# A cross-attention block in fp32: the two key halves of the probabilities are added first in 18 of 32 attention units, not 16, and the program's order is laid out anew

## The chip, the cores and the metric

The kernel runs on one core of one Trainium2 chip. The metric is the time of one execution on the device in microseconds (us). Three runs of the kernel before gave 653.56, 655.43 and 656.57 us; their median, 655.43 us, is the time before. The engines are called as the profile calls them: PE (matrix multiplication; PEld is its weight load), DVE (vector engine), ACT (scalar engine), POOL (GpSimd), and SP, which here only issues transfers (DMA). SBUF is the on-chip memory that all engines use, PSUM the banks into which PE writes.

## The reference

One transformer block without self-attention, on x of 8 x 256 x 512 and a context of the same shape, all in fp32, 16 heads of width 32:

```
x1  = layer_norm(x);  q = x1 @ q_w + q_b;  k = ctx @ k_w + k_b;  v = ctx @ v_w + v_b
s   = softmax(q @ k^T / sqrt(32), over the 256 keys)           per batch and head
hid = (s @ v) @ cproj_w + cproj_b + x
out = hid + gelu(layer_norm(hid) @ fc_w + fc_b) @ proj_w + proj_b      inner width 2048
```

The softmax is computed as exp(score - row maximum), then a product with the values, then a division by the row's sum of exponentials.

## The kernel before, in words

**Stages.** The batches are treated in two groups g of four (1024 tokens each). Each group goes through projections (k, v, q), attention, the output projection o, a second layer norm, and the MLP (fc, gelu, proj, named fc and pd). The products of the projections use Strassen's scheme: seven products P1 to P7 instead of eight, where sums of blocks are formed on DVE and POOL before (tiles named ..t or ..i), and the PSUM banks X, Y, W of a product are added into the result by DVE or copied by ACT after (operations named _t, _c). Group 1's projections lie among the attention of group 0, and the attention of group 1 lies among the o and fc products of group 0, so that PE has something else to do while the softmax of a unit runs on the other engines.

**An attention unit** is one batch and four heads, named by three digits: group, head group, batch. So 003 is group 0, head group 0, batch 3; there are 32 units. `scores` (operations s, ev, mx, mc, fold, mf, md, mm, less, exp, ss) makes on PE the scores with keys on the partitions, in two halves kc of 128 keys (8 matmuls that use 32 rows of the array each, "row" form). ACT copies them out with the mask (ev, line 614). DVE finds the row maxima (mx, L1033; fold, L1040; mf, L1042), with three small copies by ACT between (mc, L1039). The maxima are stored to DRAM (md, L594) and loaded back into all partitions (mm, L588). DVE or POOL subtract them (less, L1053 or L1057), ACT takes the exponential (exp, L1060). `attend` (av) then makes the product of probabilities and values, 8 matmuls that use 32 columns ("col" form), and the row sums, as a product with ones. There are two kinds of unit. In a p unit the product with ones runs over both key halves:

```
sums_ = [(lambda j=j: tile_of(av)[j * HD : (j + 1) * HD, 256:512], lambda: ones,
          lambda j=j, kc=kc: at(pt[j // 2], 2 * kc + j % 2), kc == 0) for kc in range(2) for j in range(4)]
```

In a z unit the two halves are first added on DVE or POOL into a tile ss (two operations ss_0, ss_1 of 128 x 512, L625), and the product with ones runs once over the sum, four matmuls in place of eight. The table KINDS says which unit is which, in the order in which the units stand.

**Order, engines and places** are written out by hand in two long tables of words. PROGRAM gives the one order in which all operations are issued, and after a colon the engine of an operation that has a choice (V DVE, A ACT, G POOL). Each engine, SP included, runs its operations strictly in that order; an operation that must wait holds up what stands behind it on its engine. PLACES gives the buffer slot of every tile: a slot holds one tile after the other, and an operation that writes a tile waits until the last reader of the slot's tile before is done. A wait on a slot is as binding as one on data. Tiles of kind Q have an even number and two halves of kind P, so that slot 54 names the Q tile there as well as its first half.

**Weights of the fc and pd products** are loaded again for each group by SP (names fl and pl, lines L588). For the fc product of group g, half s, outer product p, four loads fl{g}{s}{p}_0 to _3 are made: _2 carries the operands of the inner products P5 and P6, _3 those of P7 and P3. So fc011 is the product of group 0, half 1, p = 1; its P6 needs fl011_2, its P7 needs fl011_3.

The profile's line numbers are those of the program below; nearly all products are recorded on line 634, all additions on 625, all loads on 588 and all stores on 594.

Of the kernel before, what the change touches and what calls it, by code (L numbers as in the profile page):

```python
# [122 lines left out]
cq0_00_0 turn_c0_10_0 turn_c0_00_0 vw00 c0_10_0:A c0_00_0:V small v0_0_P1a cq0_00_1 cq0_01_1 vw10 vws3:G cq0_01_0 cq0_11_0  # L123
cq0_11_1 turn_c0_00_1 turn_c0_10_1 c0_00_1:V kw00 c0_10_1:A v0_0_P1b v0_1_P1a turn_c0_11 v0_1_P1b vw11 c0_11:A
turn_c0_01 c0_01:A turn_c0_31 cq0_10_1 cq0_10_0 vws1:G turn_c0_21 kw10 xt0_1 fw0_00_1 fw0_00_0 k0_0_P1 c0_31:A kw11
vw01 c0t1:V v0_0_t1:A vws2:V fw0_11_1 c0_21:A k0_1_P1 c0t2:V rows1 v0_1_t1:A c0t3:V fw0_11_0 turn_c0_30 turn_c0_20
v0_0_P6 xt0_0 fw0i1_3:G rows6 c0_30:V c0_20:A c0t4:V v0_1_P6 fw0i1_1:V v0_0_P2 v0_1_t2:V fw0i1_2:G fw0i4_1:V v0_1_P5
v0_0_t2:A v0_0_P5 fw0i1_4:V v0_0_t3:A kws1:G kws3:G fw0_10_1 stats_x0_00 fw0_10_0 vws4:V rows3 fw0s1:V fw1_00_1
fw0i4_3:G fw0s3:V rows0 rows7 v0_1_t3:A rows2 mk rows8 fw0s2:V rows4 mk~1 v0_1_P2 rows5 v0_0_P3 fw0i4_2:G xt0_4
v0_1_P3 xt0_6 cols kws2:V xt0_3 xt0_5 v0_0_c12:A cols~1 k0_0_t1:A fw0i5_3:V xt0_2 stats_x0_10 fw0i6_3:G fw0i5_1:G  # L130
fw0_01_1 stats_x0_20 fw0i6_1:V stats_x0_11 aggr_x0_11 fw0_01_0 xt0_7 fw0i5_2:G k0_1_t1:A fw1_00_0 fw0i5_4:G fw0i7_1:G
stats_x0_31 kw01 k0_1_P7 fw0i4_4:V fcd0_7_False aggr_x0_31 fw0i7_2:G fw0i6_2:V aggr_x0_00 fw0s4:V k0_0_P6 fw0i3_3:G
fw1_11_1 k0_0_P7 aggr_x0_10 stats_x0_01 aggr_x0_01 k0_1_P6 fw1_01_0 fw1_11_0 fcd0_6_False aggr_x0_20 eps_x0_1 v0_1_c11
stats_x0_30 pow_x0_1 aggr_x0_30 fw0i6_4:G fcd0_6_True k0_0_t2:A k0_0_P5 xt1_3 nb_x0_1 eps_x0_0 k0_1_t2:A k0_1_P5
stats_x0_21 k0_1_P2 fcd0_3_False fcd0_5_True aggr_x0_21 kws4:G k0_0_t3:A fw0i7_3:G eps_x0_3 pow_x0_0 k0_0_c22
k0_1_t3:A fw1i4_1:V eps_x0_2 pow_x0_3 nb_x0_3 fw0i7_4:V qw00 k0_1_c11 k0_0_P3 norm_x0_31:A fw0i2_3:V k0_1_c22 k0_0_P2
k0_1_P3 norm_x0_30:V pow_x0_2 fw1i4_2:V fw0i2_1:V k0_0_c11 norm_x0_10:V norm_x0_11:A fw1_01_1 nb_x0_0 fw1i4_3:V
fw1i4_4:G fw0i2_2:V nb_x0_2 norm_x0_00:V fcd0_1_True v0_1_c12:V k0_0_P4 norm_x0_01:A fw0i2_4:G fcd0_5_False fw1i1_1:G
k0_1_P4 norm_x0_20:A qw10 k0_1_c12:V k0_0_c21 k0_0_c12:A norm_x0_21:A v0_0_c11 turn_x0_10 x0_10:V qw11 fw1i1_3:G
turn_x0_31 fw0i3_1:G turn_x0_00 qw01 turn_x0_11 x0_00:A x0_11:A x0_31:V cb1_12 turn_x0_01 turn_x0_21 turn_x0_30  # L140
turn_x0_20 x0_20:A x0_01:V fcd0_2_True fw1i1_2:V qws1:V fcd1_4_True qws3:G q0_0_P1 fw0i3_2:G x0_21:A fw1i1_4:V x0t1:V
q0_1_P1 cb1_11 x0_30:A q0_0_P2 fw1i2_1:V fw0i3_4:V fw1i2_2:V x0t3:V fw1i2_3:V kd0_0_21 q0_0_t1:A qws2:V q0_0_c11
q0_0_P7 s000 kd0_0_11 kd0_0_12 xt1_2 stats_x1_11 q0_1_t1:A ev000_20 x0t2:V q0_0_P6 fw1_10_0 cb1_03 fw1_10_1
fcd1_1_True cb1_00 ev000_01 x0t4:V cb1_13 fw1i2_4:V ev000_10 fcd0_7_True q0_1_P6 ev000_31 ev000_00 fcd1_2_True
ev000_11 q0_0_t2:A q0_0_P5 q0_0_t3:A ev000_21 fw1s1:V fw1s3:V fw1s2:V fw1s4:V aggr_x1_11 q0_0_c22 ev000_30 mx000_1
q0_1_t2:A cb1_10 fcd0_3_True fcd1_5_False cb1_02 mx000_0 qws4:G fw1i3_1:G mc000_1 mc000_3 q0_1_P2 fw1i7_3:G q0_0_P4
# [1367 lines left out]
```

## Time and profile before

| | before |
|---|---|
| time, median of 3 (us) | 655.43 (653.56 to 656.57) |
| the profiled execution's own time (us) | 654.56 |
| its span, first to last instruction (us) | 652.6 |
| PE busy | 644.3 us (99%) |
| DVE busy | 581.6 us (89%) |
| ACT busy | 346.7 us (53%) |
| POOL busy | 393.5 us (60%) |
| DMA, mean | 144.83 MB, 222 GB/s |

The shares are means over stages of different kinds. A row of the view of groups reads: line, engine, operation, output <- inputs, sizes and count | busy us, mean ns of one | idle time before. A row of the timeline reads: start, length, engine, line, operation, count, and in brackets the idle time before it with what ended it. The granted PE clock is 1.00 in every stretch of the span. A tile's slot can bear the name of the first tile that lay in it, so that a load of fc weights may be printed as a load into xn_y, k or xt.

### The profile page before, as it was taken

Reading aid. Unit: us, or ns where it says so; the run is one execution under the profiler, and the core shown is the slowest. Engines: PE = TensorE matmul, PEld = TensorE weight load, DVE = VectorE, ACT = ScalarE, POOL = GpSimd, SP = SyncE. Lnnn points to the kernel's source line nnn. Section 1 sums busy time; section 2 is a strip of 40 time slices with the busy share of each in tenths; the row PEclk is TensorE's granted clock in tenths of the full one; section 3 lists DMA queues with packets and bytes.
Section 4 is the critical chain, followed back from the end, with each engine's and each line's share of the span. In section 5 each row is a group of like instructions: output and inputs, shape, how many; then the busy total and the mean of one; then the engine's idle time right before and its main releaser. Section 6 shows DMA issues by size and latency. Waiting matters only on the chain.

```text
span 652.6 us, 11265 instructions
## 1 busy us (share of the span) xinstructions
PE 644.3 (99%) x3793; PEld 487.4 (75%) x3793; DVE 581.6 (89%) x981; ACT 346.7 (53%) x711; POOL 393.5 (60%) x355
## 2 busy tenths in 40 slices
PE   9999999999999999999999999999999999999997
PEld 7845454477445676777787888888888888888886
DVE  2889999999989999999999999998878879988676
ACT  3235588999999889865884655030030232632000
POOL 2653687869997897598859765233263334512740
PEclk9999999999999999999999999999999999999999
DMA  8799998679673567786886588989979988567775
GB/s 280 232 341 313 291 263 295 224 207 153 192 237 111 159 213 217 263 264 214 247 252 193 182 262 264 298 282 230 178 196 222 219 228 191 159 171 201 204 131 98
DMA packets 206713, 144.83 MB, mean 222 GB/s; under 512 B 117136, under 2 KB 167104, under 8 KB 206656
## 3 DMA queue, kind: packets, MB, share of 16 engines
q1 hardware_dynamic: 206656, 144.11, 78.1%
q8 instruction: 30, 0.49, 0.3%
q14 instruction: 27, 0.22, 0.1%
HBM read 104.10 MB, written 39.98 MB: 221 GB/s over the span
## 4 chain that ended last, share of the span: by engine, by line
PE 60%; DMA 1%; ACT 0%; DVE 0%; issue 0%
PE fc_X L634 15%; PE pd_X L634 15%; PE fc_W L634 7%; PE pd_W L634 7%; PE pd_Y L634 4%; PE fc_Y L634 4%; PE av L634 2%; PE o_X L634 2%; PE s L634 1%; PE o_W L634 1%; DMA xn_y<-fcd 1%; PE ps_y L722 1%; PE o_Y L634 1%; ACT xn_y L822 0%; PE pd_V L634 0%; PE ps_o L1322 0%
## 5 line engine op out<-in xcount | busy, mean ns | idle before, releaser
L614 ACT ACTIVATE pr<-s,cols 128x256 f32<-128x256 f32 x256 | 103.7, 483 | 19.5 <-PE s L634 17.3
L1057 POOL TENSOR_TENSOR pr<-pr,mm 128x512 f32<-128x512 f32 x72 | 94.2, 1336 | 5.1 <-DMA mm<-md 5.1
L1033 DVE TRANSPOSE_TENSOR_REDUCE mx<-pr 128x32 f32<-128x1024 f32 x64 | 76.8, 1219 | 1.9 <-ACT pr L614 1.7
L1060 ACT ACTIVATE pr<-pr 128x1024 f32<-128x1024 f32 x64 | 66.8, 1067 | 8.9 <-POOL pr L1057 8.1
L1237 ACT ACTIVATE h<-h,cols 128x256 f32<-128x256 f32 x128 | 54.4, 498 | 31.0 <-DVE h L625 30.9
L625 DVE TENSOR_TENSOR h<-fc_X,h 128x512 f32<-128x512 f32 x80 | 52.3, 674 | 4.9 <-PE fc_X L634 4.5
L625 POOL TENSOR_TENSOR ss<-pr 128x512 f32<-128x512 f32 x24 | 32.0, 1344 | 15.4 <-ACT pr L1060 13.8
L625 DVE TENSOR_TENSOR h<-fc_W,h 128x512 f32<-128x512 f32 x48 | 31.8, 676 | 5.3 <-PE fc_W L634 5.1
L1053 DVE TENSOR_TENSOR pr<-pr,mm 128x1024 f32<-128x1024 f32 x28 | 35.2, 1275 | 0.0
L1039 ACT COPY mx<-mx 32x64 f32<-32x64 f32 x96 | 23.3, 243 | 12.2 <-DVE mx L1033 10.7
L623 POOL TENSOR_TENSOR z1i<-h,z1i 128x512 f32<-128x512 f32 x8 | 10.8, 1367 | 21.8 <-PE pd_X L634 16.4
L601 ACT COPY h<-fc_X 128x512 f32<-128x512 f32 x13 | 7.5, 593 | 29.6 <-PE fc_X L634 29.6
L634 PE MATMUL fc_W<-y1i,fl 128*128 128x256 f32 x88 | 22.1, 379 | 0.0
L1040 DVE TENSOR_REDUCE mx<-mx 32x32 f32<-32x256 f32 x32 | 18.5, 578 | 3.3 <-ACT mx L1039 3.1
L606 ACT ACTIVATE e<-pd_X,cols 128x256 f32<-128x256 f32 x7 | 3.3, 473 | 32.5 <-PE pd_X L634 32.5
L634 PE MATMUL pd_X<-z0i,pl 128*128 128x256 f32 x88 | 20.3, 379 | 0.0
L811 POOL TENSOR_TENSOR rs_y<-rs_y,neg_half 128x2 f32<-128x2 f32 x8 | 7.3, 918 | 18.7 <-DVE rs_y L808 11.4
L634 PEld LDWEIGHTS fc_W<-y1i,fl 128*128 128x128 f32 x88 | 16.7, 190 | 2.3
L634 PEld LDWEIGHTS pd_X<-z0i,pl 128*128 128x128 f32 x88 | 16.7, 190 | 2.3
L634 PE MATMUL fc_X<-y1i,fl 128*128 128x256 f32 x72 | 18.1, 381 | 0.0
L1428 POOL TENSOR_TENSOR hid<-hid,cb 128x1024 f32<-128x1024 f32 x6 | 16.5, 2768 | 2.5 <-DVE a1t L625 1.8
L625 DVE TENSOR_TENSOR po<-pd_W,po 128x256 f32<-128x256 f32 x24 | 9.9, 413 | 9.0 <-PE pd_W L634 8.9
(619 smaller groups left out, 1861.9 us busy)
## 6 DMA issues: line engine op xcount, KB each, us to landing
mm<-md SPq DMA_DIRECT2D x32, 512.0 KB, 4.6
pl<-prd SPq DMA_DIRECT2D x49, 256.0 KB, 3.5
fl<-fcd SPq DMA_DIRECT2D x46, 256.0 KB, 3.7
fw<-in_L_xattn_fc_w_dram SPq DMA_DIRECT2D x16, 256.0 KB, 6.5
hid<-in_x_dram SPq DMA_DIRECT2D x8, 512.0 KB, 3.7
pw<-in_L_xattn_proj_w_dram SPq DMA_DIRECT2D x32, 128.0 KB, 3.8
hd<-hid SPq DMA_DIRECT2D x8, 512.0 KB, 4.7
fcd<-fw0i SPq DMA_DIRECT2D x7, 512.0 KB, 5.2
```

The costliest lines, as they stand in the source:

```text
L614: lambda e: nc.scalar.activation(to(), of_(), AF.Identity, bias=bias(), scale=1.0))
L623: nc.gpsimd.tensor_tensor(to()[:, ts(k, 512)], in0()[:, ts(k, 512)], in1()[:, ts(k, 512)], op)
L625: E[e].tensor_tensor(to(), in0(), in1(), op)
L634: nc.tensor.matmul(o(), l(), r(), start=first, stop=True, skip_group_check=True)
L1033: T.op(f"mx{u}_{h}", [("DVE", 1.126)], [(pr[h], None)], [(mx, [h])], lambda e, h=h: nc.vector.tensor_reduce(tile_of(mx)[:, 0:64].rearrange ...
L1039: lambda e, a=a: nc.scalar.copy(tile_of(mx)[0:32, 64 * a : 64 + 64 * a], tile_of(mx)[32 * a : 32 * a + 32, 0:64]))
L1040: T.op(f"fold{u}", [("DVE", 0.38)], [(mx, [0, 1, 2, 3, 4])], [(mx, [5])], lambda e: nc.vector.tensor_reduce(tile_of(mx)[0:32, 256:288], ti ...
L1053: nc.vector.tensor_tensor(p_, p_, m_[:, None, :].to_broadcast([P, 2, 512]), ALU.subtract)
L1057: E[e].tensor_tensor(p_, p_, m_, ALU.subtract)
L1060: lambda e, h=h: nc.scalar.activation(tile_of(pr[h]), tile_of(pr[h]), AF.Exp), table="exp")
L1237: lambda e, f=f, b=b, c=c: nc.scalar.activation(at(h[f][b], c), at(h[f][b], c), AF.Gelu_apprx_tanh, bias=col(c_fcb + f * 4 + c), scale=1.0 ...
L1428: lambda e, v=v: E[e].tensor_tensor(v(), v(), cb.t[:, None, :].to_broadcast([P, 2, D]), ALU.add), lock=True)
```

## The change

Units 003 and 023 (the 11th and 12th of group 0) become z units. That takes 8 matmuls with ones from PE (4 in each), and adds 4 additions of 128 x 512 (ss003_0, ss003_1, ss023_0, ss023_1), all on DVE. The tables PROGRAM and PLACES are written anew as a whole, with the same operations otherwise: of those with a choice of engine 22 go from DVE to ACT, 17 from ACT to DVE, 53 from POOL to DVE and 58 from DVE to POOL. In instructions PE has 8 fewer matmuls, DVE 6 instructions fewer (7 fewer of 128 x 1024), ACT 5 more, POOL 12 more (16 more of 128 x 512, 4 fewer of 128 x 256).

```diff
 PROGRAM = """
...
-q1_1_P4 q1_1_c11 s110 pw0i1_4:G fold122 ev110_10 a0t3:G ev110_20 ev110_01 ev110_11 ev110_00 mx120_1 o0_0_t1 mf122
...
+ss001_0:V ev031_30 less003_1:V xb1_31 xT1_00 v1_1_P3 ev031_31 exp021_0 xb1_32 xb1_30 v1_1_P2 mc011_2 v1_1_c21 mx031_1
+xT1_01 xb1_33 xb1_21 att012 ss021_1:G ev031_00 v1_1_c12:V xb1_20 exp003_1 less003_0:G mc011_1 fold011 x1_00:A v1_0_P4
+exp003_0 x1_01:A v1_0_c21 ss003_1:V av001 ku033 ss003_0:V ss021_0:G ev031_11 ev031_10 s013 mf011 q1_0_P1 xT1_31 xT1_21
...
+q1_1_c11 pw0i1_3:V pw0_10_00 s110 mc122_1 q1_1_P4 mm100 pw0i1_2:V less100_0:V o0_1_t1 mc102_1 mc102_2 mc102_3 fold102
...
 PLACES = """
...
-mv_y0_0=8 rs_y0_0=5 xn_y0_00=51 xn_y0_01=6 st_y0_1=6 mv_y0_1=1 rs_y0_1=9 xn_y0_10=0 xn_y0_11=39 st_y0_2=1 mv_y0_2=7
...
-h0_01=18 fl011_0=83 fl011_1=83 fl011_2=6 fl011_3=18 fc011_X=1 fc011_Y=0 fc011_W=6 fl006_0=16 fl006_1=9 fl006_2=69
...
+mm122=72 av100=7 r100=10 rc100=5 att1_00=42 s110_0=0 s110_1=2 s110_2=3 s110_3=7 pr110_0=54 pr110_1=50 mx110=1 mm110=88
...
+y0i1=78 fc001_X=5 h0_00=58 fc001_Y=6 h0_10=30 fc001_W=2 h0_11=18 h0_01=14 fl011_0=38 fl011_1=74 fl011_2=54 fl011_3=66
...
-KINDS = ("zzzzzzzzzzpppppp", "ppppppppppzzzzzz")
+KINDS = ("zzzzzzzzzzzzpppp", "ppppppppppzzzzzz")
```

What the new order moves is shown at three places.

**DVE, ahead of the scores of unit 110** (the tile that q_1_Y is added into is the q of that unit: operation q1_1_c11; pw0i are weight sums for pd, the row L1053 is less100_0). DVE before:

```order
L1033 TENSOR_REDUCE mx_2247<-pr_0_2174 128x2x16
L625 TENSOR_TENSOR att_11_1287<-av_2205,r_2253 128x256
L625 TENSOR_TENSOR pw0i_2197<-pw_00_2056 128x256
L1053 TENSOR_TENSOR pr_0_1993<-pr_0_1993,mm_2278 128x1024
L625 TENSOR_TENSOR pw0i_2197<-pw0i_2197,pw_00_2056 128x256
L1040 TENSOR_REDUCE mx_2247<-mx_2247 32x32
L625 TENSOR_TENSOR hid_1_2092<-o_1_X,hid_1_2092 128x2x256
L1042 STREAM_TRANSPOSE mx_2247<-mx_2247 32x32
L625 TENSOR_TENSOR xt_3_497<-q_1_Y,xt_3_497 128x512
```

DVE at the same place in the changed order:

```order
L625 TENSOR_TENSOR att_11_1327<-av_2192,r_2237 128x256
L1033 TENSOR_REDUCE mx_2262<-pr_0_2126 128x2x16
L1033 TENSOR_REDUCE mx_2262<-pr_1_2142 128x2x16
L625 TENSOR_TENSOR v_1_21_362<-q_1_Y,v_1_21_362 128x512
L625 TENSOR_TENSOR pw0i_2247<-pw_00_1906 128x256
L625 TENSOR_TENSOR pw0i_2247<-pw0i_2247,pw_00_1906 128x256
L1053 TENSOR_TENSOR pr_0_1982<-pr_0_1982,mm_2303 128x1024
L625 TENSOR_TENSOR hid_1_2190<-o_1_X,hid_1_2190 128x2x256
```

The addition of q_1_Y now stands ahead of the two pw0i sums, the subtraction, the addition into hid and the two small reductions. On PE the scores of unit 110 stand one product earlier, ahead of q1_1_P4 instead of behind it.

**ACT, ahead of the last exponential of unit 033** (L614 on s is ev, L614 on att is the bias ab0, L606 is a copy of a q product; the last row is exp033_1; the rows with pr_0_2063 and pr_1_2109, or pr_0_2126 and pr_1_2142 after the change, belong to unit 122). ACT before:

```order
L614 ACTIVATE pr_0_2063<-s_1_2043,cols 128x256 x2
L1060 ACTIVATE pr_1_1700<-pr_1_1700 128x1024
L606 ACTIVATE kws_368<-q_1_X,cols 128x512
L1039 COPY mx_2076<-mx_2076 32x64 x3
L614 ACTIVATE pr_1_2109<-s_2_2045,cols 128x256
L614 ACTIVATE pr_1_2109<-s_3_2047,cols 128x256
...
L1060 ACTIVATE pr_1_1812<-pr_1_1812 128x1024
L1060 ACTIVATE pr_0_1832<-pr_0_1832 128x1024
L614 ACTIVATE att_00_1069<-att_00_1069,cols 128x512
L1060 ACTIVATE pr_0_1882<-pr_0_1882 128x1024
L1060 ACTIVATE pr_1_1879<-pr_1_1879 128x1024
```

ACT up to the same exponential in the changed order:

```order
L1039 COPY mx_2019<-mx_2019 32x64 x2
L614 ACTIVATE att_10_1136<-att_10_1136,cols 128x512
L614 ACTIVATE att_01_1404<-att_01_1404,cols 128x512
L1039 COPY mx_2019<-mx_2019 32x64
L1060 ACTIVATE pr_0_1803<-pr_0_1803 128x1024
L614 ACTIVATE pr_0_2126<-s_0_2105,cols 128x256
L614 ACTIVATE pr_0_2126<-s_1_2107,cols 128x256 x2
L614 ACTIVATE att_11_1327<-att_11_1327,cols 128x512
L1060 ACTIVATE pr_1_1705<-pr_1_1705 128x1024
L1060 ACTIVATE pr_0_1916<-pr_0_1916 128x1024
L614 ACTIVATE pr_1_2142<-s_3_2111,cols 128x256
L1060 ACTIVATE pr_1_1921<-pr_1_1921 128x1024
```

Between the first ev of unit 122 and exp033_1 ACT had 8 ev, 5 exp, 3 mc, 1 ab0 and 1 copy of a q product; now it has 12 ev (four of the next unit, 102, among them), 5 exp, 3 mc and 3 ab0.

**SP, around the weights of fc011** (the rows that load from fcd_1_102 are fl011_2 and fl011_3; md_193 is md101, the store of the maxima of unit 101). Before, fl011_3 stands here on SP, fourteen transfers ahead of fl011_2:

```order
L588 DMA mm_2680<-md_191 128x1024
L588 DMA xn_x_01_564<-fcd_1_102 128x512
L588 DMA fl_0_2695<-in_L_xattn_fc_w_dram 128x2x256
L594 DMA hd_117<-hid_0_2194 128x2x512
L594 DMA hd_117<-hid_1_2092 128x2x512
```

SP in the changed order, from fl011_2 to fl011_3, eleven transfers on:

```order
L588 DMA fl_2_2811<-fcd_1_102 128x512
L588 DMA fl_1_2816<-in_L_xattn_fc_w_dram 128x256
L594 DMA prd_116<-pw0s_2788 128x4x256
L588 DMA xn_y_00_2707<-fcd_1_94 128x512
...
L588 DMA fl_0_2705<-fcd_6_99 128x512
L594 DMA hd_117<-hid_1_2190 128x2x512
L594 DMA md_193<-mx_2859 32x32
L588 DMA xn_y_20_2908<-fcd_1_102 128x512
```

fl011_3 went from well ahead of the store md101 to right behind it. In the same way fl002_0, the first weights of fc002, stood ahead of the store md121 and stands now right behind it. The slot of fl011_2 was 6, which held xn_y0_01 before (read by the transposes of the second layer norm); now it is 54, which held probabilities of unit 110.

661 lines of the change are left out of this document (329 added, 332 removed).

## The prediction

> **What bounds the kernel now.** I read the busy shares first, then what PE waited for, then the stretches in which that happened.
>
> ```profile
> PE 644.3 (99%) x3793; PEld 487.4 (75%) x3793; DVE 581.6 (89%) x981; ACT 346.7 (53%) x711; POOL 393.5 (60%) x355
> ```
>
> PE is busy for 644.3 of 652.6 us. Only less work on PE, or fewer of its waits, can shorten the run. Its waits, all seven rows of that view (us in total, times, longest):
>
> ```profile
> PE fc_X L634 <- DMA xn_y<-fcd: 1.4, 1, 1.4
> PE s L634 <- DVE xt L625: 1.3, 1, 1.3
> PE first L646 <- DVE warm L641: 1.0, 1, 1.0
> PE ps_c L722 <- DMA cq<-in_ctx_dram: 0.4, 1, 0.4
> PE o_W L634 <- ACT pr L614: 0.3, 1, 0.3
> PE s L634 <- DVE att L625: 0.2, 1, 0.2
> PE ps_y L722 <- ACT xn_y L822: 0.2, 1, 0.2
> ```
>
> Two waits of 1.4 and 1.3 us stand out. The start (1.0 and 0.4) opens in the new order with the same rows, and I leave it alone. Where the others could grow is told by the stretches of 25 us (columns: length; busy us of PE, PEld, DVE, ACT, POOL with counts; clock, DMA share, GB/s):
>
> ```profile
> 150.00:175.00 25.00, 24.83 (x201) 16.70 (x194) 24.14 (x43) 24.73 (x52) 23.35 (x20) 1.00 0.83 173
> 175.00:200.00 25.00, 25.00 (x168) 11.73 (x170) 22.07 (x34) 24.61 (x51) 22.03 (x13) 1.00 0.69 220
> 200.00:225.00 25.00, 23.41 (x208) 16.10 (x200) 24.74 (x41) 22.11 (x53) 22.98 (x17) 1.00 0.30 93
> ```
>
> Between 150 and 200 us ACT is full (24.73 and 24.61 of 25), from 200 to 225 DVE is (24.74), and POOL is not far off (22.03 to 23.35). PE is just fed in time there by engines that have no spare time. So a new order gives no sure gain: what it shifts in one place is felt in another. The clock is 1.00 and plays no part.
>
> **Part 1: the product with ones.** Rows of the PE timeline: a z unit (ss,ones), then the p unit 003 (pr,ones), which is one of the two that change.
>
> ```profile
> 166.17 0.61 PE L634 MATMUL av<-ss,ones 128*32 128x256 f32 x8
> 166.60 1.05 PE L634 MATMUL av<-pr,vw 128*32 128x256 f32 x16
> 167.68 4.11 PE L634 MATMUL q_X<-x,qw 128*128 128x512 f32 x8
> 171.72 1.15 PE L634 MATMUL s<-xn_x,ku 32*128 32x256 f32 x16
> 172.79 1.07 PE L634 MATMUL av<-pr,ones 128*32 128x256 f32 x16
> 173.68 1.04 PE L634 MATMUL av<-pr,xt 128*32 128x256 f32 x16
> 174.66 0.70 PE L634 MATMUL q_X<-x1t,qws 128*128 128x512 f32 x1
> ```
>
> Matmuls overlap, so I take starts: 166.60 - 166.17 = 0.43 us for 8 records, 173.68 - 172.79 = 0.89 for 16. A unit that changes kind saves 0.43 to 0.46; two save **0.9 us**. This lies on PE's own path and is kept unless something else ends later.
>
> **Part 2: changes of form.** From the same rows, with 0.86 us (twice 0.43) as the work of 16 such records: row to col costs 172.79 - 171.72 - 0.86 = 0.21, col to full 174.66 - 173.68 - 0.86 = 0.12. PE's order has 90 changes of form before and 93 after: one row to col fewer, one row to full, one col to full and two full to col more. Row to full I price like row to col, full to col, which no row here isolates, between 0 and 0.21, at 0.1. Together -0.21 + 0.21 + 0.12 + 0.2 = **+0.3 us** (0.1 to 0.5).
>
> **Part 3: the four additions on DVE.** The answer on the tile ss gives what one costs (ns, min/median/max):
>
> ```profile
> L625 POOL TENSOR_TENSOR ss<-pr x24: 1260/1274/2255, 91.2 to 371.7; 128x512 f32<-128x512 f32 x24
> L625 DVE TENSOR_TENSOR ss<-pr x8: 672/690/1074, 101.6 to 371.2; 128x512 f32<-128x512 f32 x8
> ```
>
> 4 x 0.69 = 2.8 us of DVE between 150 and 185 us. DVE's idle time from 150 to 200, 0.9 + 2.9 us by the stretches, covers it: **0**. Without that cover it is 2.8 us.
>
> **Part 4: the DMA wait of 1.4 us goes.** It is that of fc011_P6 (y0i products) on its weights. The chain of waits has the load (start, length):
>
> ```profile
> 255.57 6.26 DMA xn_y<-fcd
> ```
>
> fl011_2 could not be issued before the transposes of the second layer norm had read slot 6, and took 6.26 us. Now its slot 54 is freed by av110, in PE's order ahead of the transposes, and on SP it stands three places behind mm132. It should be there in time: **-1.4 us** (bounds -1.4 and 0).
>
> **Part 5: the DVE wait of 1.3 us goes.** DVE's timeline, POOL's, and the page's row of the maxima, ahead of the scores s110:
>
> ```profile
> 208.67 0.40 DVE L625 TENSOR_TENSOR pw0i<-pw 128x256 f32<-128x256 f32 x1
> 209.00 2.29 DVE L1053 TENSOR_TENSOR pr<-pr,mm 128x1024 f32<-128x1024 f32 x1
> 211.21 1.49 DVE L625 TENSOR_TENSOR pw0i<-pw0i,pw 128x256 f32<-128x256 f32 x1
> 213.86 0.64 DVE L625 TENSOR_TENSOR xt<-q_Y,xt 128x512 f32<-128x512 f32 x1
> ```
>
> ```profile
> 210.95 1.47 POOL L623 TENSOR_TENSOR a0t<-att,a0t 128x512 f32<-128x512 f32 x1 [0.74 <-ACT att L614]
> ```
>
> ```profile
> L1033 DVE TRANSPOSE_TENSOR_REDUCE mx<-pr 128x32 f32<-128x1024 f32 x64 | 76.8, 1219 | 1.9 <-ACT pr L614 1.7
> ```
>
> The addition of q_Y ran at 213.86, behind 5.2 us of work that began at 208.67. In the new order it stands ahead of all that and behind one maximum more (1.2 us): 4.0 us sooner. The scores stand one q product sooner, 2.0 us (two q_X products, quoted above, went from 167.68 to 171.72). The 2.0 us that are left cover the 1.3 that PE waited: **-1.3 us** (bounds -1.3 and 0).
>
> Here the trace also shows DVE and POOL in each other's way: the addition of 0.40 us took 1.49 while POOL ran. The Trainium skill, "SBUF — State Buffer", section "SBUF: two separate sides", has the read and write ports that both share as an exclusive lock, held for a whole instruction when a DVE operation has two SBUF inputs. By that rule the four new additions could each be held up by a POOL instruction, 4 x 1.27 = 5.1 us, 1.3 us more than DVE's idle time there, and the sum would be 1.3 us higher. The rows for ss (median 0.69, least 0.67) show most such additions unhindered, so I go by them.
>
> **Part 6: ACT ahead of av033.** ACT's rows up to exp033_1, which ends at 201.5, while av033 begins on PE at 202.78 (PE's row av<-pr,ones):
>
> ```profile
> 191.41 1.61 ACT L614 ACTIVATE pr<-s,cols 128x256 f32<-128x256 f32 x4
> ...
> 193.79 0.77 ACT L606 ACTIVATE kws<-q_X,cols 128x512 f32<-128x512 f32 x1
> 194.58 0.75 ACT L1039 COPY mx<-mx 32x64 f32<-32x64 f32 x3
> ...
> 198.67 0.73 ACT L614 ACTIVATE att<-att,cols 128x512 f32<-128x512 f32 x1
> 199.32 2.19 ACT L1060 ACTIVATE pr<-pr 128x1024 f32<-128x1024 f32 x2
> ```
>
> ```profile
> 202.78 1.05 PE L634 MATMUL av<-pr,ones 128*32 128x256 f32 x16
> ```
>
> From 191.41 to 201.51 are 10.1 us, with 1.27 us to spare. The new order puts four ev (0.37 each, from 1.61 for four with a tail) and two ab0 (199.32 - 198.67 = 0.65 each) more into this stretch, and one copy (194.58 - 193.79 = 0.79) less: +1.5 + 1.3 - 0.8 = +2.0 us. PE's work between s122 and av033 is nearly as before (six products, one score). 2.0 - 1.27 = 0.7 late; ACT also has x1_30 more ahead of it and no idle time to make that up (24.61 of 25), so up to 1.5. I take **+1.0 us** (0 to 1.5).
>
> **Part 7: a new wait on SP.** fl011_3, needed by fc011_P7, stands now right behind md101. Rows of SP's timeline, of PE's, of the transfers from 255 to 275 us (the last number: us to landing) and of the page's transfers:
>
> ```profile
> 264.09 0.32 SPq L594 DMA_DIRECT2D md<-mx  x1
> 270.36 1.03 PE L634 MATMUL fc_W<-y0i,xn_x 128*128 128x256 f32 x4
> kw<-fcd SPq DMA_DIRECT2D x1, 256.0 KB, 8.0
> fl<-fcd SPq DMA_DIRECT2D x46, 256.0 KB, 3.7
> ```
>
> md101 was issued at 264.09, P7 began at 270.36. md101 waits for the maxima of unit 101 from DVE, which is full up to 225 us and has little room to make them sooner. Issued at 264.09 + 0.4, the load has 5.9 us until P7; without the waits of parts 4 and 5 PE comes up to 2.7 us sooner, of which part 6 gives 1 back, so about 4.2 remain. A load of this size takes 3.7 us in the median of the page and 8.0 in the stretch from 255 to 275. With 3.7 it is in time, with 8.0 PE waits 3.8; at 5.7, between the two, it waits **+1.5 us** (0 to 3.8).
>
> **Part 8: waits that nobody can name.** Everything from 150 to 350 us is as tight as the stretches say, and the order is new throughout. Below, the 0.7 us of the smaller waits (0.3, 0.2, 0.2) could go; above, waits of the size of the two largest, 1.3 and 1.4, could come. I take **+0.8 us** (-0.7 to +2.7).
>
> **The sum:** -0.9 + 0.3 + 0 - 1.4 - 1.3 + 1.0 + 1.5 + 0.8 = 0.0 us. It stands against the profiled execution, 654.56 us with its span of 652.6, which was 0.87 us below the median of the three runs; on the scale of that median it gives 655.4 us.
>
> **The rivals.** (a) **The gains stay:** parts 1, 2, 4 and 5 hold, nothing new waits and the small waits go: -0.9 + 0.3 - 1.4 - 1.3 - 0.7 = -4.0, 651.4 us. For it speaks that both large waits are moved out of their places; against it the full ACT and DVE.
> (b) **Loads behind maxima, slower:** fl011_3 waits behind md101, and fl002_0, needed by fc002_P2, stands behind md121 in the same way. DVE cannot bring the maxima forward, so each transfer that takes longer than its 4.2 us holds PE up for the rest. At 7.0 us, between the two rows of part 7, that is 2.8 at each place, 5.6 in place of part 7's 1.5: 655.4 + 4.1 = 659.5 us. From 6.6 us on (2 x 2.4 - 1.5 = 3.3) it makes the run slower. For it speaks the 8.0, against it the median of 3.7.
> (c) **ACT bounds 150 to 200:** parts 3 and 6 at their upper end, with the DVE additions waiting for the exponentials: +0.5 in part 6 and a quarter of part 3's 2.8: 656.6 us.
> (d) **The change does not do what it says:** PE's col products overlap in fours, and a half product with ones might leave the interval as it is. The 0.43 us of the z unit speaks against it; +0.9, 656.3 us.
>
> **How the numbers follow.** What can be told from no change here is 0.5%, 3.3 us: below 652.1 is faster, above 658.7 slower. Chances: forecast 0.52 (653 to 658 alone), (a) 0.14, (b) 0.18, (c) 0.12, (d) 0.04. Faster is (a), 0.14; slower is (b), 0.18; the rest, 0.68, is the same. The predicted time is 655.4 us; the range reaches to (a) and (b): 651.5 to 659.5 us.
>
> **What would show it.** Right: 144 records of av<-ss,ones in place of 128 (18 units of 8), 224 of av<-pr,ones in place of 256; no wait of fc011_P6 (fc_X) for its weights; s110 without a wait for DVE; a wait of some tenths to 1.5 us at av031 or av033 for ACT (exp, L1060); a wait of PE at the product fc011_P7 (fc_W) for a load from fcd. Wrong: if PE's waits fall below 3 us in all, (a) holds and part 7 is mis-sized; if they pass 9 us, (b) or a wait that I did not name.

## The result, and the profile after

The changed kernel takes 660.87 us (median of 19 runs, 655.66 to 662.97) against 655.01 us (median of 19, 652.60 to 656.63) for the kernel before. The ratio, estimated from all runs of both kernels (here and below it is not the quotient of the medians), is 1.0078, 95% interval 1.0064 to 1.0092: slower by about 5 us. The forecast was 655.4 us, no change, with a range up to 659.5. The kernel is slower, and its time lies outside the range.

The profiled execution of the changed kernel took 661.05 us, its span 659.3 us against 652.6 before. The busy shares, and the first five of PE's ten waits (us in total, times, longest):

```profile
PE 647.8 (98%) x3777; PEld 488.2 (74%) x3777; DVE 579.2 (88%) x975; ACT 350.2 (53%) x716; POOL 404.6 (61%) x367
```

```profile
PE av L634 <- ACT pr L1060: 3.3, 3, 2.8
PE o_X L634 <- DVE hid L625: 1.8, 1, 1.8
PE first L646 <- DVE warm L641: 1.0, 1, 1.0
PE k_W L634 <- DVE mx L1042: 0.6, 1, 0.6
PE s L634 <- DVE k L625: 0.4, 1, 0.4
```

Both waits that the profile of the kernel before shows are gone (1.4 us for a load, 1.3 us at s110), and no row names a DMA. Two larger ones have come: 2.8 us ahead of av013 at 203 us, and 1.8 us ahead of o1_1_P6 at 386 us. So I looked at what DVE and POOL did just before. The timeline of the changed kernel, DVE, then POOL, then PE (start, length, engine and line, operation, count; in brackets the idle time before it):

```profile
194.69 0.43 DVE L625 TENSOR_TENSOR att<-av,r 128x256 f32<-128x256 f32 x1
195.03 6.68 DVE L1053 TENSOR_TENSOR pr<-pr,mm 128x1024 f32<-128x1024 f32 x2
201.63 2.36 DVE L1033 TRANSPOSE_TENSOR_REDUCE mx<-pr 128x32 f32<-128x1024 f32 x2
...
204.96 0.65 DVE L625 TENSOR_TENSOR vw<-q_W,vw 128x512 f32<-128x512 f32 x1
```

```profile
194.97 5.66 POOL L1428 TENSOR_TENSOR hid<-hid,cb 128x1024 f32<-128x1024 f32 x2 [0.58 <-DMA hid<-in_x_dram]
```

```profile
205.75 1.07 PE L634 MATMUL av<-pr,ones 128*32 128x256 f32 x16 [2.79 <-ACT pr L1060]
```

The two mask subtractions of unit 013 (less013_1 and less013_0) take 6.68 us on DVE, where one alone takes 1.2. POOL adds the projection bias to the hidden state at the same time (xb0_2 and xb0_3, L1428) and needs 5.66 us for two additions of 2.36 each. Taken one by one, the four instructions run strictly in turns: xb0_2 until 197.32, less013_1 until 198.40, xb0_3 until 200.62, less013_0 until 201.70. Everything behind them on DVE is over 4 us late, down to q1_0_c21 (the row at 204.96), which empties the PSUM bank that av013 writes into (PLACES gives bank 7 to q1_0_W and to av013). PE gets that bank at 205.61 and goes on at 205.75.

The view gives the wait to ACT. But the two exponentials that av013 needs ended at 199.50 and 203.08; the one that ended at 205.72 is that of another unit. The same wait in a later run (the POOL instruction in halves, below) is put down to DVE's vw row.

The same thing happens at 384 us, with both engines on the bias addition (xb1_3 on DVE, xb1_2 on POOL). DVE, POOL, PE:

```profile
384.03 3.38 DVE L1428 TENSOR_TENSOR hid<-hid,cb 128x1024 f32<-128x1024 f32 x1
387.33 0.68 DVE L625 TENSOR_TENSOR hid<-o_X,hid 128x512 f32<-128x512 f32 x1
```

```profile
383.70 2.62 POOL L1428 TENSOR_TENSOR hid<-hid,cb 128x1024 f32<-128x1024 f32 x1 [0.88 <-DMA hid<-in_x_dram]
```

```profile
388.06 1.99 PE L634 MATMUL o_X<-vws,a1t 128*128 128x256 f32 x8 [1.79 <-DVE hid L625]
```

In the kernel before, DVE loses nothing in the same stretch. Only one subtraction of unit 013 stood on DVE there. It began 0.5 us ahead of POOL's additions, so that POOL was the one held up (its first addition took 2.92 us in place of 2.36), and what followed on DVE did not mind POOL. DVE's two bias additions of group 1 (374 and 379 us) took 1.21 and 1.22 us there. DVE and POOL of the kernel before at 192 us:

```profile
192.01 1.18 DVE L1053 TENSOR_TENSOR pr<-pr,mm 128x1024 f32<-128x1024 f32 x1
193.12 0.44 DVE L1083 TRANSPOSE_TENSOR_REDUCE rc<-av 128x8 f32<-128x256 f32 x1
```

```profile
192.51 5.24 POOL L1428 TENSOR_TENSOR hid<-hid,cb 128x1024 f32<-128x1024 f32 x2 [0.63 <-DMA hid<-in_x_dram]
```

Which of DVE's instructions mind POOL is told by the answers on the tiles mx, h and pr of the changed kernel (least, median and greatest ns):

```profile
L1033 DVE TRANSPOSE_TENSOR_REDUCE mx<-pr x64: 1190/1223/1246, 69.0 to 355.1; 128x32 f32<-128x1024 f32 x64
L625 DVE TENSOR_TENSOR h<-fc_X,h x80: 636/679/694, 288.1 to 581.1; 128x512 f32<-128x512 f32 x80
L1053 DVE TENSOR_TENSOR pr<-pr,mm x28: 1171/1212/3377, 93.0 to 373.7; 128x1024 f32<-128x1024 f32 x28
```

The 64 maxima, with one input from SBUF, are never lengthened, nor are the 80 additions that read one input from PSUM and one from SBUF. The 28 subtractions, with two inputs from SBUF, range from 1.17 to 3.38 us.

**Theory.** The loss comes from the new layout: it makes DVE's two-input instructions coincide with POOL's, each shuts the other out for a whole instruction, and PE waits for DVE. **Rivals:** (B) DVE is late because of its four new additions, or because the engines' sums have changed; (C) ACT, full from 125 to 175 us (24.60 and 24.73 us busy in two stretches of 25), sets the pace.

### The profile page after: what moved, and what is told of

The parts are those of the page before. It is cut to its first block, busy times and chain, and to the rows that moved or that the text cites. A ratio compares the mean times of both kernels' runs of the same rounds, so it can differ in the third digit from the quotient of the medians.

```text
span 659.3 us, 11222 instructions
## 1 busy us (share of the span) xinstructions
PE 647.8 (98%) x3777; PEld 488.2 (74%) x3777; DVE 579.2 (88%) x975; ACT 350.2 (53%) x716; POOL 404.6 (61%) x367
## 5 line engine op out<-in xcount | busy, mean ns | idle before, releaser
L614 ACT ACTIVATE pr<-s,cols 128x256 f32<-128x256 f32 x256 | 103.5, 483 | 10.6 <-PE s L634 7.1
L1057 POOL TENSOR_TENSOR pr<-pr,mm 128x512 f32<-128x512 f32 x72 | 90.8, 1295 | 4.1 <-DMA mm<-md 4.1
L1053 DVE TENSOR_TENSOR pr<-pr,mm 128x1024 f32<-128x1024 f32 x28 | 40.6, 1467 | 0.0
L623 POOL TENSOR_TENSOR z1i<-z1t,z1i 128x512 f32<-128x512 f32 x6 | 7.5, 1278 | 34.5 <-DVE z1i L625 27.0
L634 PE MATMUL fc_X<-y1i,fl 128*128 128x256 f32 x104 | 25.8, 380 | 0.0
L634 PEld LDWEIGHTS fc_X<-y1i,fl 128*128 128x128 f32 x104 | 19.7, 190 | 2.9 <-issue 0.3
L606 ACT ACTIVATE e<-pd_X,cols 128x256 f32<-128x256 f32 x7 | 3.3, 471 | 32.8 <-PE pd_X L634 31.8
L634 PE MATMUL pd_X<-z1i,pl 128*128 128x256 f32 x88 | 20.6, 381 | 0.0
L625 POOL TENSOR_TENSOR h<-h,e 128x512 f32<-128x512 f32 x8 | 10.6, 1336 | 13.4 <-DVE e L625 13.4
L634 PE MATMUL av<-pr,ones 128*32 128x256 f32 x224 | 15.5, 383 | 3.3 <-ACT pr L1060 3.3
L634 PEld LDWEIGHTS pd_X<-z1i,pl 128*128 128x128 f32 x88 | 16.6, 190 | 2.7 <-DVE po L625 0.3
```

Of the source, the lines that this page charges most:

```text
L614: lambda e: nc.scalar.activation(to(), of_(), AF.Identity, bias=bias(), scale=1.0))
L623: nc.gpsimd.tensor_tensor(to()[:, ts(k, 512)], in0()[:, ts(k, 512)], in1()[:, ts(k, 512)], op)
L625: E[e].tensor_tensor(to(), in0(), in1(), op)
L634: nc.tensor.matmul(o(), l(), r(), start=first, stop=True, skip_group_check=True)
L1053: nc.vector.tensor_tensor(p_, p_, m_[:, None, :].to_broadcast([P, 2, 512]), ALU.subtract)
L1057: E[e].tensor_tensor(p_, p_, m_, ALU.subtract)
```

## The experiments

Unless a run says otherwise the kernels are complete. Line numbers of some experiments lie one or two lower than those above. A word of PROGRAM that moves stands in the diffs with its neighbour.

**1. POOL's side cut out (e1_short_adds).**

```diff
+            few = 8 if (g, b) in ((0, 2), (0, 3), (1, 2)) else D
-                 lambda e, v=v: E[e].tensor_tensor(v(), v(), cb.t[:, None, :].to_broadcast([P, 2, D]), ALU.add), lock=True)
+                 lambda e, v=v, few=few: E[e].tensor_tensor(v()[:, :, :few], v()[:, :, :few], cb.t[:, None, :few].to_broadcast([P, 2, few]), ALU.add), lock=True)
```

> The changed kernel, with three of POOL's additions of the projection bias to the hidden state (xb0_2 and xb0_3 at 195, xb1_2 at 384 us) cut to 8 columns of each 512; the rest of that bias is left out, every other instruction stays. Theory A (VectorE and POOL shut each other out): the two mask subtractions on VectorE that took 3.38 us each go back to 1.2, TensorE's 2.8 us wait ahead of av013 and its 1.8 us wait ahead of o1_1_P6 both go, and the evictions that ScalarE had late behind them come earlier too (0.6 us at s102, 0.8 at s120): the span falls by 4.5 to 6 us, to about 654, a ratio of 1.000 against the kernel before. Rival B (VectorE is late since it has the four new half-sum adds, 2.7 us, and more of the engines' work): those adds are all still there, so VectorE is as late as it was; less than 1 us is gained, ratio 1.007. Rival C (ScalarE, 98 per cent busy from 125 to 175 us, sets the pace): the waits move to ScalarE's evictions, gain 1 to 2 us, ratio about 1.005.

Measured: 653.96 us, ratio 0.9993 (0.9975 to 1.0011), span 651.6. DVE and POOL at the same place, and all that PE still waited for over 0.2 us:

```profile
194.07 2.37 DVE L1052 TENSOR_TENSOR pr<-pr,mm 128x1024 f32<-128x1024 f32 x2
196.36 2.36 DVE L1032 TRANSPOSE_TENSOR_REDUCE mx<-pr 128x32 f32<-128x1024 f32 x2
```

```profile
193.98 1.38 POOL L1428 TENSOR_TENSOR hid<-hid,cb 128x16 f32<-128x16 f32 x2 [0.54 <-DVE mx L1041]
```

```profile
PE first L645 <- DVE warm L640: 1.0, 1, 1.0
PE k_W L633 <- DVE att L624: 0.4, 1, 0.4
PE s L633 <- DVE k L624: 0.4, 1, 0.4
PE av L633 <- ACT pr L1059: 0.3, 1, 0.3
```

The pair of subtractions is back at 2.37 us and both waits are gone. The ratio fell from 1.0078 to 0.9993, by 0.85% or 5.6 us. DVE's work is untouched, so B falls for this layout. ACT's is too; C falls as the main cause. POOL's own work has become less, though, so this run alone cannot tell a meeting from a POOL that is late; runs 4 and 9, which leave each engine's sum as it was, can.

**2. The change of form alone (e2_before_halved).** The kernel before with

```diff
-KINDS = ("zzzzzzzzzzpppppp", "ppppppppppzzzzzz")
+KINDS = ("zzzzzzzzzzzzpppp", "ppppppppppzzzzzz")
+exp003_1 ss003_1:V   mx031_0 ss003_0:V   mx033_0 ss023_1:V   q1_0_c22 ss023_0:V
-exp003_0, behind q1_1_P1
+exp003_0, ahead of ev013_11
+ss003=82 ss023=30
```

> The kernel before with the change of form alone: units 003 and 023 also add their key halves (four adds on VectorE, one exponential moved ahead of one eviction, two free places), order, engines and places otherwise as before. Theory A: the form by itself pays what the prediction gave it, 16 records fewer (0.9 us) less 0.3 us or less for changes of form, and the loss of the changed kernel comes from the new layout; the span falls by 0.4 to 0.9 us, ratio 0.999. It can lose that again where the 1.3 us of adds at 184 us bring a mask subtraction on VectorE to run beside POOL's bias additions at 192 us: then a subtraction takes up to 3.4 us and TensorE waits up to 2 us, ratio up to 1.002. Rival B (the new adds on VectorE are what makes it late): the kernel gets slower by 2 us or more, ratio 1.003 or above, with the wait behind VectorE in 195 to 215 us and without a lengthened instruction there.

Measured: 658.01 us, ratio 1.0049 (1.0035 to 1.0062): 3.2 us slower, outside what theory A gave it. Rival B has the sign, but not the mechanism. DVE, POOL and PE around unit 023:

```profile
185.88 1.35 DVE L624 TENSOR_TENSOR ss<-pr 128x512 f32<-128x512 f32 x1
187.15 0.68 DVE L624 TENSOR_TENSOR v<-q_W,v 128x512 f32<-128x512 f32 x1
187.75 1.15 DVE L624 TENSOR_TENSOR ss<-pr 128x512 f32<-128x512 f32 x1
188.83 2.30 DVE L1052 TENSOR_TENSOR pr<-pr,mm 128x1024 f32<-128x1024 f32 x1
```

```profile
185.40 1.28 POOL L624 TENSOR_TENSOR qw<-v,ow 128x512 f32<-128x512 f32 x1
186.63 5.64 POOL L1056 TENSOR_TENSOR pr<-pr,mm 128x512 f32<-128x512 f32 x3
```

```profile
188.96 0.64 PE L633 MATMUL av<-ss,ones 128*32 128x256 f32 x8 [1.30 <-DVE ss L624]
```

The new additions themselves meet POOL and take 1.35 and 1.15 us in place of 0.68; the two of unit 003 take 1.65 and 0.87. The subtraction behind them takes 2.30, and PE waits 1.3 us for the second addition. That is less than half of the loss: PE also waits 0.8 us at 170 us for ACT, and smaller waits have grown. Here the additions, with the exponential that is moved for them, cost more than the product saves. The prediction had them hidden.

**3. The layout alone (e3_after_unhalved).** The changed kernel with

```diff
-KINDS = ("zzzzzzzzzzzzpppp", "ppppppppppzzzzzz")
+KINDS = ("zzzzzzzzzzpppppp", "ppppppppppzzzzzz")
-ss003_0:V ss003_1:V ss023_0:V ss023_1:V
```

> The changed kernel with its layout kept and the change of form taken back: units 003 and 023 run the product with ones over both key halves again, their four half-sum adds on VectorE (2.7 us in all) are gone. Theory A: TensorE has 0.9 us more, and the collision at 195 us stays, since the fold of unit 033 ahead of the mask subtractions waits for ScalarE until 192.95 us whether the adds are there or not; TensorE's wait ahead of av013 is still 2 to 3 us and the one at 384 us still 1.8; ratio 1.007 to 1.010. Rival B (the adds are what makes VectorE late): VectorE is 1.3 us ahead at 188 us and 2.7 in all, the wait at 201 us falls below 1 us and the kernel gains 1 to 2 us on the changed one, ratio 1.004 to 1.006.

Measured: 659.75 us, ratio 1.0079 (1.0061 to 1.0097), the same as with the additions. In its trace the pair of subtractions takes 6.13 us from 194.40 on and PE waits 2.8 us ahead of av013; in this execution the meeting at 384 us did not come about. The layout carries the loss without the change of form.

**4. The meetings taken out by order (e4_order_mended).** The changed kernel with

```diff
-less031_0:G   less013_1:V
+less031_0:V   less013_1:G
-a1t2:V gelu0_201 gelu0_033 gelu0_303 xb1_3:V o1_1_t1
+a1t2:V gelu0_201 gelu0_033 gelu0_303 o1_1_t1
-fc013_c21 gelu0_122
+fc013_c21 xb1_3:V gelu0_122
```

> The changed kernel, complete, with two collisions taken out by order alone: of the four mask subtractions at 189 to 202 us, less031_0 goes back to VectorE and less013_1 back to POOL as the kernel before had them, so that only one is left on VectorE when POOL adds the bias; and the bias addition xb1_3 on VectorE stands behind three of its additions for the projections, so that it meets POOL's xb1_2 no more. Theory A: the wait ahead of av013 falls from 2.8 us to under 0.5, the one ahead of o1_1_P6 from 1.8 to 0, and ScalarE's late evictions behind the first give up to 1 us more: gain 4 to 6 us on the changed kernel, ratio 0.999 to 1.002. Rival B: VectorE's sum is unchanged, so its lateness is too; gain under 1 us. Rival C (ScalarE sets the pace from 125 us): gain 1 to 2 us, ratio about 1.005.

Measured: 656.19 us, ratio 1.0005 (0.9985 to 1.0024), as theory A had it. The twelve times run from 652.62 to 662.57, and the profiled execution is the shortest of them (span 650.8). In it the first meeting is small, and a later one has come about, between the subtractions of unit 033 and xb0_3:

```profile
192.84 1.61 DVE L1052 TENSOR_TENSOR pr<-pr,mm 128x1024 f32<-128x1024 f32 x1
...
199.12 3.33 DVE L1052 TENSOR_TENSOR pr<-pr,mm 128x1024 f32<-128x1024 f32 x2
```

So the order took away the two large meetings and made a smaller one elsewhere. Order fixes who comes after whom on one engine. Where two engines meet can also hang on when a load lands: in the changed kernel and in the one before, what released POOL's first bias addition is a DMA (the brackets of POOL's rows above).

**5. POOL's instruction in halves (e5_pool_in_halves).** The changed kernel with

```diff
-                 lambda e, v=v: E[e].tensor_tensor(v(), v(), cb.t[:, None, :].to_broadcast([P, 2, D]), ALU.add), lock=True)
+                 lambda e, v=v: [E[e].tensor_tensor(w, w, c, ALU.add) for w, c in
+                                 ([(v()[:, i], cb.t) for i in range(2)] if e == "POOL" else [(v(), cb.t[:, None, :].to_broadcast([P, 2, D]))])], lock=True)
```

> The changed kernel, complete, with one edit: where POOL adds the bias to the hidden state, it does so in two instructions of 512 columns (some 1.28 us each by POOL's other rows of that size) in place of one of 1024 (2.36 us). Theory A (each of VectorE and POOL shuts the other out for one whole instruction): at 195 us the turns are then 1.28 and 1.2 us, the two mask subtractions end 1.7 to 1.8 us earlier (4.9 us for the pair in place of 6.7) and TensorE's wait ahead of av013 is about 1.0 us in place of 2.8; at 384 us VectorE's addition ends 1.3 us earlier and the wait ahead of o1_1_P6 is about 0.5 in place of 1.8. Gain about 3 us, ratio about 1.003. Rival B (the two engines share the port by halves, each instruction slowed by the other's traffic for as long as they overlap): the work of both is the same, so the ends and the waits stay; gain under 0.5 us.

Measured: 656.66 us, ratio 1.0012 (0.9997 to 1.0028), 0.66% less than the changed kernel. DVE, POOL, and PE's wait for the bank:

```profile
196.27 4.54 DVE L1052 TENSOR_TENSOR pr<-pr,mm 128x1024 f32<-128x1024 f32 x2
```

```profile
196.24 6.93 POOL L1427 TENSOR_TENSOR hid<-hid,cb 128x512 f32<-128x512 f32 x4 [0.60 <-DMA hid<-in_x_dram]
```

```profile
PE av L633 <- DVE vw L624: 1.3, 1, 1.3
```

The same work in smaller instructions: the pair takes 4.54 us in place of 6.68 (4.9 expected), the wait 1.3 in place of 2.8 (1.0 expected). Had the two engines slowed each other by halves, the pair would have ended no sooner; how long one instruction shuts the other out goes by its length. At 384 us DVE came first and was not held up, so that place says nothing here. The profiled execution is the longest of the twelve (664.79 us): PE also waits 2.7 us at k1_0_P4 (120 us), and 4.1 us at 240 us, which the last section looks at.

**6. The kernel before, without its two waits (e6_before_mended, then e9_before_mended_place).**

```diff
-q1_1_c11, behind less100_0:V pw0i1_2:V fold102 o0_1_t1 mf102
+q1_1_c11, ahead of less100_0:V
-fl011_2, behind pw0_01_00 pw0_01_10 fl001_3 pw0_01_01 pw0_01_11
+fl011_2, ahead of pw0_01_00
```

> The kernel before, complete, with its two largest waits of TensorE taken out by order alone: the eviction q1_1_c11 stands on VectorE ahead of less100_0 and pw0i1_2 (which meet POOL's a0t2 at 209 to 213 us), and the load fl011_2 ahead of four loads of 128 KB on the queue of SP. The prediction put the gains of the change at these two places at 1.3 and 1.4 us. If they hold by themselves, the span falls by 2 to 2.7 us, ratio 0.996 to 0.997. If the work behind them has no slack (the next evictions and the next load late by as much), less than 1 us is left, ratio 0.999 or above.

Measured: 657.88 us, ratio 1.0032 (1.0013 to 1.0050). The edit does more than it should: slot 6 still held a layer-norm tile that the transposes were to read, and with the load ahead of them they waited for it and read weights in its place. That part of the computation is changed, and PE waits there:

```profile
255.95 0.48 PE L721 MATMUL ps_y<-ident,xn_y 128*128 128x128 f32 x1 [3.04 <-DMA xn_y<-fcd]
```

The wait at s110 is gone in it. The second kernel gives the load a place that is free by then:

```diff
-fl011_2=6
+fl011_2=86
```

> The kernel before, complete, with its two largest waits of TensorE taken out: the eviction q1_1_c11 on VectorE ahead of less100_0 and pw0i1_2, and the load fl011_2 ahead of four loads of 128 KB, now in a place that is free by then (86 in place of 6, whose last reader ends at 255 us). Theory: the two gains of the prediction (1.3 and 1.4 us) are real and independent of the change; the run with the old place showed the first of them, less 0.45 us at the next eviction. Span 2 to 2.6 us shorter, ratio 0.996 to 0.997. If work behind them has no slack, ratio 0.999 or above.

Measured: 654.04 us (652.01 to 655.11), ratio 0.9981 (0.9966 to 0.9995). Both waits are gone (no row for DMA, none for xt); the waits that are left:

```profile
PE first L645 <- DVE warm L640: 1.0, 1, 1.0
PE s L633 <- DVE att L624: 1.0, 2, 0.7
PE fc_X L633 <- DVE h L624: 0.7, 1, 0.7
```

This is faster than both kernels, by 1.2 us rather than by 2 to 2.6. The two waits of 0.7 us, at a score (312 us) and at an fc product (316 us), are not in the profile of the kernel before, but they are no price of the mend: runs 2, 7 and 9 have them at the same two operations, and they keep fl011_2 in its old order and slot. PE doesn't wait for that load in them either (in run 7 it was issued at 255.87 us, and fc011_P6 began without a wait at 260.73). So the 1.4 us for the load stands in one execution of the kernel before and in none of these three kernels, and where it is missing PE waits about as long for DVE further on. The 1.2 us that are left fit the wait at s110 alone.

**7. The saving on PE alone (e7_half_sums).** The kernel before, in which the product with ones of units 003 and 023 runs over one key half only.

```diff
-at(pt[j // 2], 2 * kc + j % 2), kc == 0) for kc in range(2) for j in range(4)]
+at(pt[j // 2], 2 * kc + j % 2), kc == (1 if u in ("003", "023") else 0)) for kc in range(1 if u in ("003", "023") else 0, 2) for j in range(4)]
```

> The kernel before, in which units 003 and 023 run the product with ones over the second key half alone: 8 records of it in place of 16 in each, without the adds of the halves (the first half is left out of these two units' sums). This is the change's saving on TensorE without its price on VectorE. By the prediction's first term it is worth 0.86 us: ratio 0.9987. Set beside the run with the four adds (1.0049, 3 us slower), it puts the price of the adds in the old layout at 3.5 to 4.5 us. If it is no faster than the kernel before, TensorE was not the bound at these two units.

Measured: 655.33 us, ratio 0.9996 (0.9986 to 1.0005). The expected 0.9987 lies just inside the interval, and so does no gain at all. Against run 2, the four additions, with the exponential moved for them, cost 0.53% or 3.5 us in the old layout.

**8. Both mends together (e8_mended_halves).** The changed kernel with the edits of runs 4 and 5 and

```diff
-fold030 mx012_1 vu030 ev032_01 ev032_10 k1_0_c22
+k1_0_c22 mx012_0
```

> The changed kernel, complete, with the order mended as in the earlier run (ratio 1.0005: less031_0 on VectorE, less013_1 on POOL, xb1_3 after three projections' additions), POOL's bias additions in two instructions of 512, and the eviction k1_0_c22 ahead of the maximum mx012_0 on VectorE, which was late behind a mask subtraction that met POOL at 113 us. Theory A: what is left of the collisions shrinks from 2.4 to 1.3 us at each meeting; ratio 0.996 to 0.999, and the times lie closer together than those of the mended order (652.6 to 662.6). Rival: the collisions are not what is left, ratio 1.000 as in the mended order.

Measured: 656.90 us (654.69 to 662.17), ratio 1.0038 (1.0014 to 1.0063). A miss: not faster than run 4, and no closer together. Its profiled execution (span 654.6) has no lengthened subtraction at 195 to 202 us; there POOL was the one shut out. What makes its long executions long is not in that profile, and stays open.

**9. The meeting brought into the kernel before (e10_before_swapped).**

```diff
-less031_0:V   less013_1:G
+less031_0:G   less013_1:V, ahead of less013_0:V
```

> The kernel before, complete, with one part of the change alone: less031_0 moves from VectorE to POOL, less013_1 from POOL to VectorE, ahead of less013_0. Each engine's sum stays as it was within 0.1 us. Theory A (collision): the two subtractions on VectorE at 192 us now meet POOL's bias additions xb0_2 and xb0_3, as they do in the changed kernel; one of them takes 3.4 us in place of 1.2, VectorE is 3 us late at 196 us, and TensorE waits ahead of av033 for the exponential behind less033: 2 to 3.5 us lost, ratio 1.003 to 1.005. Rival B (the sums of the engines decide): within 0.5 us of the kernel before, ratio 1.000. Rival C (VectorE's order, not the port): the lost time is at most the 1.2 us that one more subtraction takes ahead of the rest, with no instruction lengthened.

Measured: 657.39 us, ratio 1.0034 (1.0019 to 1.0049). DVE and POOL:

```profile
191.17 4.48 DVE L1052 TENSOR_TENSOR pr<-pr,mm 128x1024 f32<-128x1024 f32 x2
```

```profile
191.82 6.06 POOL L1427 TENSOR_TENSOR hid<-hid,cb 128x1024 f32<-128x1024 f32 x2 [1.79 <-DMA hid<-in_x_dram]
```

One exchange of engines between two equal instructions costs 2.2 us. The second of the pair takes 3.3 us (4.48 less 1.2), and PE waits ahead of av031, av033 and s120. The engines' sums are as before, so it is the meeting.

**10. The change of form without meetings (e11_short_unhalved).** Run 1 with the edit of run 3.

> The changed kernel with POOL's three bias additions cut to 8 columns as in the first run (0.9993; the rest of that bias is left out) and units 003 and 023 without the adds, the product with ones over both halves again. It asks what the change of form is worth in the new layout once the collisions are out. If the adds hide on VectorE as the prediction had it, the form is worth its 0.86 us and this kernel is that much slower than the first run: ratio 1.0006. If the adds cost on VectorE and at the port what the product saves, it is the same or faster: ratio 0.999 or below.

Measured: 654.28 us, ratio 1.0002 (0.9976 to 1.0028), against 0.9993 with the additions. The difference has the sign and about the size of the 0.86 us, but the intervals overlap almost wholly: this doesn't settle it. The times run from 652.96 to 662.62 us although POOL's three additions are cut, so these three meetings alone are not what spreads the times of the new layout (eleven of the twelve of run 1 lie between 653.1 and 655.9).

## Why the prediction was wrong, point by point

The numbers are those of one profiled execution of each kernel. The span grew by 6.7 us. I counted PE's lost time myself, as what lies between the starts of two operations beyond their records and the usual price of a change of form: 13.1 us before, 20.3 after.

| Part | predicted (us) | measured (us) | |
|---|---|---|---|
| 1. product with ones | -0.9 | -0.9 | right |
| 2. changes of form | +0.3 | +0.3 | right; it is what the other terms leave, an estimate |
| 3. additions on DVE | 0 | not told from 0 in the new layout | none of the four was lengthened here; wrong in the old layout (run 2 against run 7, 3.5) |
| 4. DMA wait at fc011_P6 | -1.4 | -1.5 | right for these two executions, by luck |
| 5. DVE wait at s110 | -1.3 | -1.4 | right |
| 6. ACT ahead of av033 | +1.0 | 0 of its own | wrong |
| 7. fl011_3 behind md101 | +1.5 | 0 | wrong |
| 8. waits that nobody can name | +0.8 | +10.1 | wrong: the step that failed |

**Parts 1, 4 and 5.** The answer on the tile av, and PE's rows of fc011_P6 and s110, which carry no wait any more:

```profile
L634 PE MATMUL av<-pr,ones x224: 376/379/404, 193.8 to 305.3; 128*32 128x256 f32 x112
L634 PE MATMUL av<-ss,ones x144: 379/379/404, 97.1 to 378.8; 128*32 128x256 f32 x144
```

```profile
218.49 1.15 PE L634 MATMUL s<-v 32*128 32x256 f32 x16
...
268.25 1.99 PE L634 MATMUL fc_X<-y0i,fl 128*128 128x256 f32 x8
```

The new z units have 16 records fewer, and at 0.43 us for 8 (the prediction's rows) these are the 0.9 us. So rival (d) falls. That the whole run gets shorter by it was not shown: run 7 can't be told from no gain. Part 5 fits the time as well (the second kernel of run 6 gained 1.2 us). Part 4 does not: the prediction took the wait from one execution, and runs 2, 7 and 9 keep the load as it was and have no such wait, as told under 6.

**Part 7 and rival (b).** The load behind md101 was issued at 270.79, and fc011_P7 began at 275.24 without a wait; loads of that kind took 3.3 us there. SP, then PE:

```profile
270.36 0.32 SPq L594 DMA_DIRECT2D md<-mx  x1
270.79 0.36 SPq L588 DMA_DIRECT2D xn_y<-fcd  x1
```

```profile
275.24 1.89 PE L634 MATMUL fc_W<-y0i,xn_y 128*128 128x256 f32 x8
```

The 4.45 us left for it were what I had worked out (4.2); the transfer time was mis-sized, since I took 5.7 between two rows. Rival (b) came near the time, by luck, and was wrong in all else: no wait of PE in this kernel is for a load.

**Part 6 and rival (c).** ACT did run late at 198 us, but as the one kept waiting:

```profile
198.44 1.06 ACT L1060 ACTIVATE pr<-pr 128x1024 f32<-128x1024 f32 x1 [1.85 <-DVE pr L1053]
```

With POOL's part cut out (run 1), PE lost 0.3 us between av033 and s120, as much as in the kernel before. The 2.0 us of work that I counted into this stretch were there, but PE waited no longer for them.

**Part 8, with part 3.** Of the 10.1 us, 3.0 are at av013 and 1.9 at o1_1_P6. Another 1.1 are ACT's evictions, late behind DVE's pair of subtractions (at s102 and s120), and 0.7 are at k1_0_P4, behind a subtraction that met POOL's c1t4 at 113 us. The remaining 3.4 are waits of 0.2 to 0.6 us, most of them for ACT's evictions, and no run took them apart one by one; but the profiled execution of run 1 is 7.7 us shorter in span than that of the changed kernel (651.6 against 659.3), so some of them may hang on the three meetings too. Two thirds (6.7) are one mechanism.

The step that failed is part 8: +0.8 us, at most +2.7, sized by the two largest waits of the kernel before. It put at nothing what the new order makes of DVE's and POOL's meetings, and by this count these cost 6.7. The prediction had the mechanism in hand: its rows showed an addition of 0.40 us taking 1.49 beside POOL, and a subtraction of 1.2 taking 2.29, and it named the rule. But it asked the rule only of the four new additions, and set it aside by the median of the ss rows. For these four that came out right in the new layout, where none of the 12 additions into ss was lengthened (the row below); in the old layout (run 2) the same four took 0.87 to 1.65 us. So it was right by luck: a median says that meetings are rare, and not what another order does to them. And the exchange of less013_1 for less031_0, which the two PROGRAM tables show, was not set beside POOL's xb0_2 and xb0_3, which run in the same stretch.

```profile
L625 DVE TENSOR_TENSOR ss<-pr x12: 637/674/693, 92.5 to 376.3; 128x512 f32<-128x512 f32 x12
```

Part 3 also has a sum that is wrong. If all four additions had been held up for 5.1 us, this would have come on top of their own 2.8, so DVE would have been 5.1 + 2.8 - 3.8 = 4.1 us late and not 1.3.

The Trainium skill, "SBUF — State Buffer", section "SBUF: two separate sides", has the port pair of SBUF that DVE and POOL share as an exclusive lock: the instruction that comes first holds it to its end and the other stands still, for DVE instructions with two SBUF inputs against POOL instructions that read SBUF. The runs agree with it in three points: the turns at 195 us fit to 0.1 us, halving POOL's instruction took the pair from 6.68 to 4.54 us, and the maxima and the additions with one SBUF input never grew.

"If PE's waits pass 9 us, (b) or a wait that I did not name" was the right question: the rows of the view add up to 8.3, just below, and it was the unnamed one.

## What to carry to other kernels

When an instruction with two SBUF inputs moves onto DVE or POOL, look up what the other of the two runs in that stretch: the price of a meeting is up to the length of the other's instruction, or of several that follow without a gap (next section), and it strikes everything behind it on its engine. Keep long two-input instructions off both engines at the same time, or split the one that is not urgent. A profile shows one execution. A wait that it shows, like the 1.4 us for a load here, may be missing in the next, and taking it away gains nothing where another wait stands behind it: look for it in a second trace before it goes into a sum.

## What the runs showed of the hardware that I had not expected

The turns are not always fair. The profiled execution of run 5 was the longest of its twelve (664.79 us against a median of 656.66). In it a DVE addition that normally takes 1.2 us stood through several POOL subtractions in a row. DVE, then POOL:

```profile
231.80 6.52 DVE L624 TENSOR_TENSOR a0t<-att,a0t 128x1024 f32<-128x1024 f32 x1
```

```profile
229.82 7.42 POOL L1056 TENSOR_TENSOR pr<-pr,mm 128x512 f32<-128x512 f32 x6
```

POOL ran its six instructions without a gap, 1.27 us each, and DVE was let in only after the last. PE waited 4.1 us for what stood behind it. At 195 us the two engines had taken turns. Why it went otherwise here no run shows. DVE was kept out for so long in this one trace only.

The other way round it is in the kernel before too. At 178.03 us a mask subtraction of POOL, which normally takes 1.27 us, took 4.09, while DVE ran one addition and two subtractions, all with two inputs from SBUF, without a gap; POOL ended 1.15 us after the last of them. In run 8 a bias addition of POOL took 4.16 us at 201 us in the same way. POOL's subtractions in the kernel before (least, median and greatest ns):

```profile
L1057 POOL TENSOR_TENSOR pr<-pr,mm x72: 1257/1273/4088, 86.2 to 313.0; 128x512 f32<-128x512 f32 x72
```

So a meeting can cost more than one instruction of the other engine. Whether this is what makes single executions several us longer than the rest is not shown.
